# List rows placed by TensorE products, another order ahead of layer 1, and earlier fetches in a three-layer max-aggregation GNN on one Trainium2 core

## The chip, the cores and the metric

The kernel runs on one core of one Trainium2 chip. The core has five engines that work side by side and meet at semaphores: TensorE (PE, matrix products; PEld is its weight load), VectorE (DVE), ScalarE (ACT), GpSimd (POOL, which here mostly issues indirect DMAs: row gathers by a list of indices) and SyncE (SP, which issues the other DMAs). The metric is device time in microseconds (us), the median over several runs. Lower is better.

## The reference, cut to what matters

There are N = 6250 nodes with 128 features and E = 200000 edges, sorted by destination; the destinations are drawn unevenly (6250 times the square of a uniform number), so that some nodes have many edges and most have few. All numbers are float32.

```python
def sage(x, src, dst, Wl, bl, Wr):
    agg = jax.ops.segment_max(x[src], dst, num_segments=x.shape[0])
    agg = jnp.where(jnp.isfinite(agg), agg, 0.0)
    return agg @ Wl + bl + x @ Wr

h = jnp.maximum(_layernorm(x, axis=-1), 0.0)
h = leaky_relu(sage(h, src, dst, Wl1, bl1, Wr1), 0.01)   # 128 -> 256
h = leaky_relu(sage(h, src, dst, Wl2, bl2, Wr2), 0.01)   # 256 -> 256
h = leaky_relu(sage(h, src, dst, Wl3, bl3, Wr3), 0.01)   # 256 -> 128
return x + h
```

## The kernel before

**Tiles and tables.** The nodes are cut into 50 tiles of 127 (`R`). Each layer's input stands in DRAM three times: as rows (`table`, for gathers), as pairs of source tiles (`pair`, 25 pairs `g`) and transposed (`across`). Destination tiles fall into four groups `k`: narrow ones (list 0, 20 tiles), eight virtual ones that hold pieces of the three tiles with the most edges (their rows are found by `virtual`, L446), the remaining 19 narrow ones, and the eight wide ones.

**The main way of an edge.** For each layer, group and source pair there is a step. ACT (or DVE, L1077) makes one-hot matrices (`hot`, L1081 and L1083) from byte indices (`idx_sb`), PE multiplies them with the pair's features (`pg`, L1112), which fetches for every destination one source row, and DVE takes the maximum into `acc` (L1127, L1129). There are 975 steps: 225 in layer 1, 375 in each of the other two. In layer 1 group 0 has steps 0 to 74, the virtual group 75 to 124, group 2 steps 125 to 199 and the wide one the rest.

**The lists.** A source pair serves at most so many edges of one destination. What is left over goes into lists: DVE picks a tile's leftover entries (`pick_rows`, L744, into `picked`), ranks the destinations by their number (`rank_rows`, L774, giving `to_i`, where a destination's entries go, and `end_i`, where its result will stand), and the entries are rearranged so that the longest lists come first and short columns need few gathers. `CAPS` says how many entries each block of 128 destinations has at most; the longest few are folded over free partitions (`fold`). Per entry column, GpSimd gathers 128 rows from `table` (`Listed.gather`, L1174), for which ACT first turns the entries into integers (`let`, L1159). DVE takes the maxima of gathered rows (L1184, L1217), and SP stores the result to `best` (L1224). Layer 1 has 517 such gathers, the others 563 each.

**How list rows are rearranged before the change.** `send_row` (L829) scatters one tile's picked entries to DRAM (`picks`) by an indirect DMA on GpSimd, with a small memset ahead of it: 59 in all, 20, 8, 19, 8 and 4 for lists 0 to 4. `load_ell` (L839) loads the result (`ell`, and its folded part `fold`) back on SP. List 0 is done ahead of layer 1; the others inside it, by chores.

**Ahead of layer 1.** 50 windows (`window`, L386, gather on POOL and count on ACT, L391) find where each tile's edges begin (`places`, L395, giving `at_i`); then `row` (L421) fetches each tile's edge columns on POOL: 39 narrow, 8 wide by `at_i`, 8 virtual by `pos_i`. LayerNorm in five blocks (`ln_...`) runs between. `expand` (L862) and `lookups` (L881) make the byte indices of group 0.

**Nodes.** When a tile's maxima are done, its list result is fetched from `best` as `agg` by POOL (`Node.fetch`, L1244; virtual ones through `Joined`, L1317), transposed on PE (`aT_p`, L1260), joined with `acc` on DVE (`mz`, L1266) and multiplied with the weights (L1271 to L1275).

**What sets the order.** The engines run in program order. The program is written step by step from an agenda: `plan(t, rank, f)` puts a piece of work into step `t`, and within a step the ranks come in a fixed order: first LET, FRESH, TURN, then half the step's products, then MAXIMA, REST, LINEAR, MERGE, SOONER, GATHER and FETCH, then the other half. Chores (masks, flags, picks, ranks, expands, lookups of the later groups) are spread over steps by `spread` (L1448). In layer 1 each gather is put on a step by a planner's clock (`step_us`), the estimated cost of a gather `POOL_US` and a head start `BEHIND_US`. Every gather waits, by an added dependency, for the last maximum written ahead of it (`maxed[-1]`).

## Time and profile before

| | |
|---|---|
| median of 3 runs | 3005.79 us (3004.02 to 3019.61) |
| the profiled execution's own time | 3018.82 us |
| its span in the trace | 3017.0 us |
| mean granted TensorE clock | 0.90 |
| DMA traffic | 594.48 MB, mean 197 GB/s |
| first list gather on POOL | starts at 199.2 us |
| layer 1's last list gather | starts at 1006.4 us |
| layer 2's first list gather | starts at 1220.7 us |

The profile is of one execution. Its groups name a line, an engine, an operation and the tiles (output, then inputs), with a count; then busy time and the mean of one in ns; then the idle time of the engine just before them and what ended most of it. "issue" is time in which the engine waited for nothing that the profile shows. Line numbers are those of the kernel before.

### The profile page before, as it was taken

To read this page: it belongs to the slowest core of one execution; us is meant where nothing else is said; L and a number is where in the kernel's file an instruction comes from. 1 tells how busy PE (TensorE), PEld (TensorE's weight loads), DVE (VectorE), ACT (ScalarE), POOL (GpSimd) and SP (SyncE) were. 2 spreads that over 40 slices of the span, in tenths; PEclk is the share of its full clock that TensorE was granted. 3 is DMA by queue.
4 is the path that set the end of the run, shared out by engine and by line. 5 is a ranking of instruction groups with operands and counts; after the bars stand their busy time and mean duration, and the time that the engine had idled before them with its cause. 6 is when DMAs were issued, how large, how long until landed. Compare 5 with 4: busy or idle time off the path is not lost.

```text
span 3017.0 us, 36583 instructions
## 1 busy us (share of the span) xinstructions
PE 2289.6 (76%) x9364; PEld 1728.3 (57%) x9365; DVE 2430.8 (81%) x4080; ACT 1812.6 (60%) x2826; POOL 2045.6 (68%) x2059
## 2 busy tenths in 40 slices
PE   2025545666656787999988999988999897899886
PEld 1023323344434555777776778766777776678664
DVE  6688856877878686889997678898899897678996
ACT  5227768745556665666665578654656665578641
POOL 6787765777677311677777767774577777767773
PEclk9996667777878898999999999999999999999997
DMA  9425544566545478667677887797667667777884
GB/s 249 146 75 135 141 119 113 156 184 202 151 135 155 151 224 251 216 196 220 201 195 226 249 262 237 241 290 252 195 211 220 195 189 212 215 224 231 245 243 129
DMA packets 378786, 594.48 MB, mean 197 GB/s; under 512 B 77438, under 2 KB 230411, under 8 KB 377929
## 3 DMA queue, kind: packets, MB, share of 16 engines
q1 hardware_dynamic: 250425, 346.88, 36.9%
q0 software_dynamic: 85312, 213.54, 25.8%
q10 hardware_dynamic: 42832, 31.64, 3.2%
q8 instruction: 78, 1.28, 0.2%
q14 instruction: 139, 1.14, 0.1%
HBM read 469.30 MB, written 122.50 MB: 196 GB/s over the span
## 4 chain that ended last, share of the span: by engine, by line
PE 31%; DMA 14%; DVE 13%; issue 7%; POOL 4%; ACT 3%; SPq 0%; DVEq 0%; POOLq 0%; ACTq 0%
PE pg L1112 26%; DVE acc L1129 7%; DMA g<-table,let 6%; DMA agg<-best,end_i 5%; POOL g L1174 4%; PE z_p L1273 2%; PE z_p L1275 2%; DVE g L1184 2%; DVE g L1217 1%; ACT away L1081 1%; DMA pair_sb<-pair 1%; ACT hot L1083 1%; DMA idx_sb<-idx 1%; PE aT_p L1260 1%; DMA agg_v<-best,end_i 1%
## 5 line engine op out<-in xcount | busy, mean ns | idle before, releaser
L1112 PE MATMUL pg<-hot,pair_sb 128*128 128x512 f32 (+2 forms) x7448 | 1984.1, 419 | 294.1 <-ACT hot L1083 118.1
L1174 POOL DMA_INDIRECT g<-table,let x1643 | 1666.7, 1014 | 621.9 <-issue 340.5
L1112 PEld LDWEIGHTS pg<-hot,pair_sb 128*128 128x128 f32 x7448 | 1448.5, 203 | 686.7 <-ACT hot L1083 222.2
L1129 DVE TENSOR_TENSOR acc<-acc,pg 128x1024 f32<-128x1024 f32 (+4 forms) x1179 | 1355.3, 1170 | 242.6 <-PE pg L1112 229.4
L1081 ACT ACTIVATE away<-idx_sb,near 128x1024 uint8<-128x1024 uint8 (+3 forms) x585 | 581.0, 993 | 83.7 <-DMA idx_sb<-idx 40.6
L1083 ACT ACTIVATE hot<-away 128x1024 fp32r<-128x1024 uint8 (+3 forms) x585 | 535.0, 915 | 156.9 <-PE pg L1112 141.0
L1083 ACT ACTIVATE hot<-idx_sb 128x1024 fp32r<-128x1024 uint8 (+3 forms) x594 | 514.2, 886 | 185.8 <-PE pg L1112 181.0
L1244 POOL DMA_INDIRECT agg<-best,end_i x141 | 150.2, 1065 | 238.2 <-PE aT_p L1260 175.8
L1277 ACT COPY s<-z_p 127x256 f32<-127x256 f32 (+1 forms) x150 | 50.2, 335 | 339.4 <-PE z_p L1275 321.0
L1217 DVE TENSOR_TENSOR g<-g 128x1024 f32<-128x1024 f32 (+5 forms) x224 | 225.6, 1007 | 33.2 <-DMA g<-table,let 29.6
L1184 DVE TENSOR_TENSOR g<-g 128x256 f32<-128x256 f32 (+3 forms) x394 | 195.7, 497 | 44.5 <-DMA g<-table,let 24.6
L1260 PE MATMUL aT_p<-ident,agg 128*128 128x128 f32 x250 | 60.2, 309 | 128.3 <-DMA agg<-best,end_i 114.4
L1275 PE MATMUL z_p<-wl,mz 128*128 128x256 f32 (+1 forms) x500 | 122.2, 362 | 31.0 <-DVE mz L1266 30.9
L1273 PE MATMUL z_p<-wr,hT_in 128*128 128x256 f32 (+1 forms) x500 | 138.6, 396 | 7.4 <-DMA hT_in<-across 7.4
L969 ACT COPY hT<-hT_p 128x254 f32<-128x254 f32 x100 | 37.1, 371 | 159.0 <-PE hT_p L967 153.1
L1260 PEld LDWEIGHTS aT_p<-ident,agg 128*128 128x128 f32 x250 | 33.9, 153 | 159.7 <-DMA agg<-best,end_i 84.5
L1266 DVE TENSOR_TENSOR mz<-acc,aT_p 128x256 f32<-128x256 f32 (+1 forms) x141 | 52.3, 371 | 84.6 <-PE aT_p L1260 84.4
L1275 PEld LDWEIGHTS z_p<-wl,mz 128*128 128x128 f32 x500 | 89.7, 208 | 44.7 <-DVE mz L1266 36.3
L1077 DVE TENSOR_SCALAR hot<-idx_sb,beyond 128x1024 fp32r<-128x1024 uint8 x144 | 102.9, 715 | 2.1 <-DMA idx_sb<-idx 2.0
L1273 PEld LDWEIGHTS z_p<-wr,hT_in 128*128 128x128 f32 x500 | 82.4, 208 | 30.1 <-DMA hT_in<-across 9.2
L1159 ACT ACTIVATE let<-ell 128x4 int32<-128x4 int16 (+3 forms) x453 | 81.4, 191 | 6.7 <-DMA g<-table,let 4.2
L831 POOL DMA_INDIRECT picks<-picked,to_i x59 | 64.3, 1089 | 20.3 <-issue 10.0
(298 smaller groups left out, 1195.3 us busy)
## 6 DMA issues: line engine op xcount, KB each, us to landing
pair_sb<-pair SPq DMA_DIRECT2D x394, 256.0 KB
idx_sb<-far SPq DMA_DIRECT2D x48, 616.0 KB
g<-table,let POOLq DMA_INDIRECT x1643
far<-away ACTq DMA_DIRECT2D x198, 128.0 KB
pair<-pr SPq DMA_DIRECT2D x98, 256.0 KB
idx_sb<-idx SPq DMA_DIRECT2D x75, 304.0 KB
idx_sb<-far SPq DMA_DIRECT2D x50, 304.0 KB
best<-g SPq DMA_DIRECT2D x118, 128.0 KB
```

Source lines behind the costliest of these rows:

```text
L1077: nc.vector.tensor_scalar(hot[:, :w], d, beyond, None, op0=OP.is_equal)
L1081: nc.scalar.activation(away, d, AF.Abs, bias=near[:, s : s + 1], scale=1.0)
L1083: nc.scalar.activation(hot[:, :w], d, AF.Relu, bias=1.0, scale=-1.0)
L1112: nc.tensor.matmul(to, pr[:, i, kk * P : (kk + 1) * P], hot[:, o : o + bw], start=((alone or s == 0) and i == 0), stop=((alone or s == sid ...
L1129: maxed.append(nc.vector.tensor_max(to, to, of))
L1174: got = nc.gpsimd.indirect_dma_start(out=self.tiles[q, b, j < 0][:, i, :], out_offset=None, in_=tables[self.layer], in_offset=bass.Indirec ...
L1184: nc.vector.tensor_max(g[:h, :n, :], g[:h, :n, :], g[:h, w - n : w, :])
L1217: nc.vector.tensor_max(base[:, : i + 1, :], base[:, : i + 1, :], g[:, : i + 1, :])
L1244: nc.gpsimd.indirect_dma_start(out=self.agg[:, : self.F], out_offset=None, in_=of, in_offset=bass.IndirectOffsetOnAxis(ap=at, axis=0),)
L1260: nc.tensor.transpose(aT_p[:, i, :], self.agg[:, i * P : (i + 1) * P], ident)
L1273: nc.tensor.matmul(z_p, self.hT[:, i, :], wr[layer][:, i, :], start=False, stop=False)
L1275: nc.tensor.matmul(z_p, self.m[:, i, :], wl[layer][:, i, :], start=False, stop=(i == K - 1))
```

## The change

It has five parts.

1. **List rows are placed by products.** `send_row` and `load_ell` go, and with them `picks`. `place` builds on DVE, for some tiles of a list at a time, a one-hot matrix of each entry's lane and, for every block of 128 destinations, the entries where the block matches and zero elsewhere. `gather_rows` multiplies the two on PE, one product a tile, summed in PSUM, and copies the sum to `ell` (float32 now, with only as many columns a block as `CAPS` allows). `fold_rows` moves the folded columns over partitions by products with shifted identities. Inside layer 1 `move` plans a placement in one step and its products in the next.
2. **Another order ahead of layer 1.** Windows are 200 wide instead of 400 (`WINS` = 8 samples), the first 20 narrow tiles have 32 columns flagged instead of 40 (`CN`). Window gathers, row fetches and LayerNorm pieces are interleaved in another order; `expand` runs for each half of group 0. List 0's rank, placement, products and fold come behind the expands, the lookups and the bias split.
3. **Work put behind the first gathers.** After 12 list gathers come the eight virtual rows, 32 gathers, and then the last six narrow and the eight wide rows. `virtual` runs in step 1, the check of windows in step 2. The floor stores on SP come behind the bias stores.
4. **Early fetches.** FETCH moves from the end of a step to its head. In layers 2 and 3 the nodes of the last group are fetched up to two steps ahead, into six buffers.
5. **Planning.** Chores of the first stretch are spread over steps 7 to 54 instead of 0 to 54. Late lookups are in two parts, the second two steps later. Layer 1's list stores are issued three steps later instead of two. In layer 1 a gather waits for the fourth last maximum instead of the last. `POOL_US` is 1.26 for 1.34, `BEHIND_US` 75 for 62, and the early gathers are counted from 24 us for 10.

```diff
-CB = 40
-WIN = 400
+CB, CN = 40, 32
+WIN, WINS = 200, 8
...
-    def send_row(k, i):
-        nc.gpsimd.memset(gap_t, 0.0)
-        s = nc.gpsimd.indirect_dma_start(
-            out=picks[k], out_offset=bass.IndirectOffsetOnAxis(ap=to_i[k][:, i : i + 1], axis=0),
-            in_=picked[k][:, i, :], in_offset=None,
...
-    def load_ell(k):
-        n = len(LISTS[k])
-        rows = picks[k].rearrange("(p q) m -> p q m", q=n)
-        nc.sync.dma_start(ell[k], rows)
...
+    def parts_of_list(k, most):
+        n, width_k = len(LISTS[k]), sum(RAGGED[k][-1])
+        m = min(n, most // max(P, width_k))
+        m = -(-n // -(-n // m))
+        return [range(i, min(i + m, n)) for i in range(0, n, m)]
+
+    def place(k, us, S, at):
+        n, W = len(us), sum(RAGGED[k][-1])
+        of = slice(us[0], us[-1] + 1)
+        hot, data = S(at[0], F32, n, P), S(at[1], F32, n, W)
+        nc.vector.tensor_tensor(
+            hot, iota_f[:, None, :].to_broadcast([P, n, P]), lane_f[:, of, None].to_broadcast([P, n, P]), op=OP.is_equal
+        )
+        for q, (o, m) in enumerate(RAGGED[k]):
+            nc.vector.scalar_tensor_tensor(
+                data[:, :, o : o + m], block_f[:, of, None].to_broadcast([P, n, m]), float(q), picked[k][:, of, :m],
+                op0=OP.is_equal, op1=OP.mult,
+            )
+        return hot, data
+
+    def gather_rows(k, us, hot, data):
+        W = sum(RAGGED[k][-1])
+        p = psum.tile([P, 512], F32, tag="t", bufs=2, name="ell_p")
+        for i in range(len(us)):
+            nc.tensor.matmul(p[:, :W], hot[:, i, :], data[:, i, :], start=(i == 0), stop=(i == len(us) - 1))
+        if us[0] == 0:
+            nc.scalar.copy(ell[k], p[:, :W])
+        else:
+            nc.vector.tensor_add(ell[k], ell[k], p[:, :W])
+
+    def fold_rows(k):
...
+                nc.tensor.matmul(
+                    p[:, to : to + b - a], moved[d][:h, :], ell[k][:h, a:b], start=(j == 0), stop=(j == len(cuts) - 1)
+                )
...
+        nc.scalar.copy(fold[k], p)
...
-            if maxed:
-                tc.add_manual_dep(got.ins, maxed[-1].ins.name, SYNC, reason="gathers keep to the steps")
+            behind = 1 if self.layer else 4
+            if len(maxed) >= behind:
+                tc.add_manual_dep(got.ins, maxed[-behind].ins.name, SYNC, reason="gathers keep to the steps")
...
-                later_on(2, lambda: nc.sync.dma_start(view[:, q, :], base[:, 0, :]))
+                later_on(2 if self.layer or q == n - 1 else 3, lambda: nc.sync.dma_start(view[:, q, :], base[:, 0, :]))
...
-            self.agg = node.tile([P, H], F32, tag="agg", name="agg", bufs=4)
+            pool, tag, n = (later, "agg_v", 6) if layer and self.k == NK - 1 else (node, "agg", 4)
+            self.agg = pool.tile([P, H], F32, tag=tag, name="agg", bufs=n)
...
+    def move(k, t):
+        for us in parts_of_list(k, 12 * P):
+            got = []
+            plan(t, MAXIMA, lambda us=us, got=got: got.extend(place(k, us, S_acc, (1, 3))))
+            plan(t + 1, MAXIMA, lambda us=us, got=got: gather_rows(k, us, *got))
+            t += 2
+        plan(t, MAXIMA, lambda: known(k))
+        return t
...
-        chores.append((2, lambda: lookups(us, got[0], s, made)))
+        chores.append((2, lambda: got.update(v=leaves(us, got[0], s, made))))
+        behind[len(chores) - 1] = lambda: lookups(us, got["v"], s, made)
...
-                plan(t + 3, MAXIMA, lambda k=k: send(k))
-                plan(t + 9, MAXIMA, lambda k=k: load(k))
-                loaded_in[k] = t + 9
+                loaded_in[k] = move(k, t + 1)
...
-    for (n0, n1), (t0, t1) in zip(itertools.pairwise(parts_at), ((0, 54), (55, 108), (110, 172))):
+    for (n0, n1), (t0, t1) in zip(itertools.pairwise(parts_at), ((7, 54), (55, 108), (110, 172))):
...
-    POOL_US, LAND_US, BEHIND_US = 1.34, 12.0, 62.0
+    POOL_US, LAND_US, BEHIND_US = 1.26, 12.0, 75.0
...
-            plan(ta, FETCH, begin(key, make))
+            plan(ta - ahead, FETCH, begin(key, make))
+            plan(ta, FETCH, lambda: accs[key].load())
...
-    soon = early_list
-    for t in range(EARLY):
-        soon.release(t)
-        soon.gather(t)
-    window_check()
     setup.close()
...
     pair_until(0)
+    load_until(0)
+    halves_of = list(zip(parts_of_list(0, 12 * P), ((1, 3), (0, 2)), strict=True))
+    rank_rows(0, S_acc, made)
+    placed = [place(0, us, S_acc, at) for us, at in halves_of]
+    for (us, _), got in zip(halves_of, placed):
+        gather_rows(0, us, *got)
+    fold_rows(0)
+
+    def early_gathers(t0, t1):
+        for t in range(t0, t1):
+            early_list.release(t)
+            early_list.gather(t)
+
+    early_gathers(0, 12)
+    plan(1, MAXIMA, lambda: virtual(lambda i: acc_t[i // 2][:, 1, i % 2 * 12 * P : (i % 2 + 1) * 12 * P]))
+    plan(2, MAXIMA, window_check)
+    plan(2, GATHER, lambda: [row(("w", NW + v)) for v in range(NV)])
+    plan(2, GATHER, lambda: early_gathers(12, EARLY))
+    plan(4, GATHER, lambda: [row(("n", i)) for i in range(NN - 6, NN)])
+    plan(8, GATHER, lambda: [row(("w", i)) for i in range(NW)])
...
-        act(LET, FRESH, TURN)
+        act(LET, FETCH, FRESH, TURN)
...
-        act(MAXIMA, REST, LINEAR, MERGE, SOONER, GATHER, FETCH)
+        act(MAXIMA, REST, LINEAR, MERGE, SOONER, GATHER)
```

Next, three places in the order of instructions. A row is a line, an operation, its output and inputs with buffer numbers, the output's shape, and how often it comes in a row.

The first is POOL from the first window to the first gathers of layer 1. Before the change, its rows up to the second of the 20 sends (`win_d` is a window, `rows_n` and `rows_w` are edge columns):

```order
L386 DMA win_d<-in_dst_dram,win_i 128x400 x23
L421 DMA rows_n<-cols,at_i 128x48 x20
L386 DMA win_d<-in_dst_dram,win_i 128x400 x27
L421 DMA rows_n<-cols,at_i 128x64 x19
L421 DMA rows_w<-cols,at_i 128x128 x8
L830 MEMSET gap_t 128x1
L831 DMA picks_160<-picked_905,to_i_910 2560x24
```

After the change, from the first window to the long run of gathers ahead of the first node's fetch:

```order
L387 DMA win_d<-in_dst_dram,win_i 128x200 x13
L422 DMA rows_n<-cols,at_i 128x48 x10
L387 DMA win_d<-in_dst_dram,win_i 128x200 x10
L422 DMA rows_n<-cols,at_i 128x48 x10
L387 DMA win_d<-in_dst_dram,win_i 128x200 x27
L422 DMA rows_n<-cols,at_i 128x64 x13
L1205 DMA g<-table_75,let 128x128 x12
L422 DMA rows_w<-cols,pos_i 128x64 x8
L1205 DMA g<-table_75,let 128x128 x32
L422 DMA rows_n<-cols,at_i 128x64 x6
L422 DMA rows_w<-cols,at_i 128x128 x8
L1205 DMA g<-table_75,let 128x128 x208
```

The sends are gone, the 50 windows are cut into three runs with row fetches between, and 22 row fetches stand behind the first 12 list gathers.

The second is SP at the loads that the first products need. Before the change, the last stores of the floors, then list 0's loads and what follows:

```order
L630 DMA joined_149<-zeros 1x128
L630 DMA joined_150<-zeros 1x256
L842 DMA ell_890<-picks_160 128x480
L849 DMA fold_895<-picks_160 64x1 x2
L849 DMA fold_895<-picks_160 32x2 x4
L902 DMA idx_152<-v_1420 25x1024 x2
L902 DMA idx_152<-v_1420 25x512
L556 DMA bias_0_1456<-b_parts 1x16x16 x3
L556 DMA bias_1_1466<-b_parts 1x16x16 x3
L556 DMA bias_2_1476<-b_parts 1x16x8 x3
L1034 DMA pair_sb<-pair_4_82 128x512 x4
L1026 DMA idx_sb<-idx_152 128x2560 x5
```

After the change, the bias stores and the first of the 23 floor and zero stores:

```order
L564 DMA bias_0_1274<-b_parts 1x16x16 x3
L564 DMA bias_1_1284<-b_parts 1x16x16 x3
L564 DMA bias_2_1294<-b_parts 1x16x8 x3
L983 DMA table_75<-floor 1x128
L983 DMA table_76<-floor 1x256
L983 DMA table_77<-floor 1x256
```

The list's loads are gone. The 23 small floor and zero stores, which came before them, now lie between the bias stores and the first four `pair_sb` loads, which follow directly behind the last of them and are followed by the five `idx_sb` loads as before.

The third is DVE where list 0 is ranked and placed after the change, ahead of step 1's virtual rows (`lane_f` and `block_f` say where an entry goes; the tiles named `acc_1342` and `acc_1343` are used as scratch here):

```order
L768 TENSOR_SCALAR rank_h<-left_n_341 128x20
L769 SCALAR_TENSOR_TENSOR rank_f<-to_i_334,rank_h 128x20
L777 TENSOR_SCALAR rank_h<-count_n 128x20
L778 TENSOR_TENSOR rank_f<-rank_f,rank_h 128x20
L780 TENSOR_SCALAR end_i_324<-rank_f 128x20
L783 TENSOR_TENSOR sums<-rank_p,lim_351 128x24
L785 TENSOR_REDUCE over<-sums 128x1
L798 TENSOR_TENSOR acc_1342<-iota_f,lane_f 128x1280
L802 SCALAR_TENSOR_TENSOR acc_1343<-block_f,picked_329 128x10x22
L802 SCALAR_TENSOR_TENSOR acc_1343<-block_f,picked_329 128x10x10
L802 SCALAR_TENSOR_TENSOR acc_1343<-block_f,picked_329 128x10x9
L802 SCALAR_TENSOR_TENSOR acc_1343<-block_f,picked_329 128x10x8 x2
```

Before the change nothing stood between the last row of the rank and the virtual rows; here two comparisons of 128x1280 elements and 44 small products do. The second half is like the one shown, but for its end: the sum of the second product is added to `ell`.

More of the change, by code (lines that the diff above doesn't have):

```diff
@@ L930 @@
     L0 = LISTS[0]
+    half = NP // 2
     list_consts()
-    half = NP // 2
+    for i, b in enumerate((bl1, bl2, bl3)):
+        bias.append(load_b(b, f"b{i + 1}", first))
+    ln_stats(4)
+    ln_stats(3)
+    some(6)
+    ln_root(4)
+    some(1)
+    ln_root(3)
+    some(6)
+    ln_rows(4)
+    places(FIRST, HALF)
+    for i in range(half):
+        row(("n", i))
+    places(0, VT)
+    some(5)
+    ln_relu(4)
+    ln_rows(3)
+    ln_stats(2)
+    some(5)
+    ln_turn(4)
+    ln_root(2)
+    ln_halves(4)
```

272 lines of the change are left out of this document (128 added, 144 removed).

## The prediction

> **What bounds the kernel now.** I read the page first, then busy time by stretches, then each engine's waits, then GpSimd's timeline. The page's first lines (busy time, share of the span, instructions), its clock line and the gather group:
>
> ```profile
> PE 2289.6 (76%) x9364; PEld 1728.3 (57%) x9365; DVE 2430.8 (81%) x4080; ACT 1812.6 (60%) x2826; POOL 2045.6 (68%) x2059
> ...
> PEclk9996667777878898999999999999999999999997
> ...
> L1174 POOL DMA_INDIRECT g<-table,let x1643 | 1666.7, 1014 | 621.9 <-issue 340.5
> ```
>
> No engine is full over the whole span, so the bound must be read stage by stage. The busy time by stretches does that; a row is the stretch, its length, busy time of PE, PEld, DVE, ACT and POOL, then clock and DMA share:
>
> ```profile
> 0.00:100.00 100.00, 17.29 (x64) 11.66 (x64) 68.92 (x369) 52.47 (x119) 66.39 (x68) 1.00 0.92 265
> 100.00:200.00 100.00, 18.59 (x85) 15.93 (x86) 69.46 (x235) 14.80 (x48) 78.72 (x89) 1.00 0.16 40
> 212.00:510.00 298.00, 151.03 (x421) 100.11 (x422) 224.39 (x707) 217.12 (x293) 208.22 (x235) 0.68 0.48 128
> 510.00:1010.00 500.00, 313.33 (x1028) 212.53 (x1027) 387.70 (x795) 278.74 (x424) 379.83 (x384) 0.78 0.56 158
> 1010.00:1190.00 180.00, 148.02 (x575) 102.07 (x573) 145.88 (x208) 131.58 (x180) 23.19 (x23) 0.91 0.74 231
> 1190.00:1605.00 415.00, 385.28 (x1618) 302.50 (x1619) 369.74 (x392) 264.67 (x423) 296.13 (x290) 0.97 0.69 206
> ```
>
> There are four kinds of stage. Setup (to about 200 us) is a chain over DVE, POOL and ACT. From there to 1010 us POOL shows 76%, but each gather is followed by about 0.30 us of issue, so it goes end to end: layer 1 there is bound by GpSimd. From 1010 to 1190 POOL is nearly empty (23 of 180) and DVE and PE set the pace. In layers 2 and 3 PE is at 93% and DVE at 89%. GpSimd's groups between 200 and 1010 us, and the spread of the gather's time there:
>
> ```profile
> L1174 POOL DMA_INDIRECT g<-table,let x517 | 521.1, 1008 | 185.8 <-issue 112.2 <-ACT hot L1083 22.1 <-DMA g<-table,let 15.2
> L831 POOL DMA_INDIRECT picks<-picked,to_i x39 | 39.4, 1011 | 17.1 <-DVE rank_h L806 9.9 <-issue 7.3
> L1174 POOL DMA_INDIRECT g<-table,let x517: 940/945/2316, 199.2 to 1006.4; - x173
> ```
>
> **The change, term by term**, against the profiled execution's 3018.82 us (span 3017.0 and 1.8 around it). That run lies 13.0 over the median 3005.79; I subtract the same difference from the median.
>
> *Setup: the first gather.* GpSimd's timeline (start, duration) around list 0 and DVE's around the virtual rows, which follow list 0's rank; then DVE's two longest waits before 230 us:
>
> ```profile
> 157.77 2.53 POOL L831 DMA_INDIRECT picks<-picked,to_i  x1
> 187.62 1.11 POOL L831 DMA_INDIRECT picks<-picked,to_i  x1 [0.15 <-issue]
> 189.03 1.12 POOL L421 DMA_INDIRECT rows_w<-cols,pos_i  x1 [0.30 <-DVE b_parts L552]
> 199.22 0.95 POOL L1174 DMA_INDIRECT g<-table,let  x1 [0.30 <-issue]
> ...
> 145.10 0.16 DVE L449 TENSOR_SCALAR nrow_i<-count_n 128x3 int32<-128x3 f32 x1
> 156.54 2.26 DVE L500 TENSOR_SCALAR starts<-iota_r,vs,has_v 128x1024 bf16<-128x1024 f32 x3
> 168.18 0.22 DVE L511 TENSOR_SCALAR by_row<-iota_f,part_f 128x8 f32<-128x8 f32 x1
> 171.32 0.16 DVE L526 TENSOR_REDUCE over<-outside 128x1 f32<-128x3 f32 x1
> ...
> DVE at_n L397 <- ACT junk_w L391: 24.3, 3, 18.2
> DVE acc L1662 <- DMA bias<-b_parts: 9.8, 1, 9.8
> ```
>
> Twenty sends (31 us) and eight row fetches (10 us) lie ahead of the first gather; all go from there. But list 0's rank now stands behind the expands, the lookups and the bias split on DVE, with two placements, 20 products and the fold behind it. DVE's work ahead of the first gather is 68.9 + 69.5 = 138 us now. The virtual rows leave it (145.1 to 158.8 and 168.2 to 171.5: 17 us), placement comes (12, below), and ten half expands for five add about 1.5, an estimate: 135. DVE stood idle 62 us of the first 200; windows half as wide shorten its wait for ACT, but now two rounds of row fetches have windows between them. I keep 68 idle: first gather at about 204, **+5**; ends 55 and 95 idle, first gather at 190 and 230 (-9 and +31).
>
> What a placement costs no row shows. Nearest rows, of DVE and, for its products, of PE:
>
> ```profile
> L361 DVE TENSOR_TENSOR pr<-hs,pr 128x1280 fp32r<-128x1280 f32 x5 | 7.4, 1475 | 2.9 <-ACT pr L346 2.9
> L793 DVE TENSOR_TENSOR scratch<-scratch,rank_p 128x500 f32<-128x500 f32 x1 | 0.7, 674 | 1.1 <-PE rank_p L792 1.1
> L398 DVE SCALAR_TENSOR_TENSOR at_n<-win_f,at_n 128x20 f32<-128x20 f32 (+2 forms) x3 | 0.5, 177 | 0.1
> ...
> L1260 PE MATMUL aT_p<-ident,agg 128*128 128x128 f32 x250 | 60.2, 309 | 128.3 <-DMA agg<-best,end_i 114.4
> ```
>
> List 0 is placed in two parts. Each has one 128x1280 comparison (1.48 us) and 22 small products over 1180 elements in all. From 20 elements at 177 ns to 500 at 674 a further element costs about 1.04 ns, so such an instruction has some 0.16 us fixed: 22 x 0.16 + 1.2 = 4.7. Together 6.2 a part, 12 for list 0. The same sum gives about 3 for list 1, 15 for list 2 (three parts), 8 for lists 3 and 4, so **38 us more DVE work** in all, 26 of it behind the first gather. The fixed part may be smaller in a row of small instructions, so I keep 25 and 38 as the ends and take 38. The 59 products are priced by the transposes (309 ns): 18 us of PE, spread over lists; PE has 147 of 298 us idle from 212 to 510, which hides all but list 0's, where about 3 us show between the second placement and the fold (inside the 68). The copies to `ell` and `fold` are ten on ACT of about 0.35 us: nothing.
>
> *GpSimd in layer 1.* Behind the first gather 39 sends go: 39 x (1.01 + 0.30) = -51. Two waits around lists go with them: 9.9 for `rank_h` above, and 19.3 here, where the last gather of list 1 and the first of list 2 stand:
>
> ```profile
> 440.99 1.09 POOL L1174 DMA_INDIRECT g<-table,let  x1 [0.30 <-issue]
> 496.50 1.25 POOL L1174 DMA_INDIRECT g<-table,let  x1 [19.32 <-ACT hot L1083]
> ```
>
> That is -29. In their place 22 row fetches come behind the first gathers (8 by `pos_i`, 6 narrow, 8 wide), 22 x 1.27 (the eight from 189.03 to 199.22 took 10.2) = +28, and after 12 gathers (15 us) POOL waits for `pos_i`, whose 17 us of DVE and 24 small products now start only at step 1: about +10. No step reads them before the late lookups, whose work now starts at step 7 and not at 0, which is their cover. With the start's +5 GpSimd alone would be through with layer 1's lists -51 - 29 + 28 + 10 + 5 = **37 us earlier**.
>
> *What DVE gives back.* Where DVE waited in layer 1, from 212 to 510 us and then from 510 to 1030:
>
> ```profile
> DVE acc L1129 <- PE pg L1112: 25.2, 8, 8.8
> DVE g L1217 <- DMA g<-table,let: 18.6, 4, 8.0
> DVE g L1184 <- DMA g<-table,let: 11.2, 5, 5.1
> ...
> DVE mz L1266 <- PE aT_p L1260: 25.9, 10, 5.8
> DVE mz L1263 <- PE aT_p L1260: 17.4, 3, 14.4
> ```
>
> Up to list 2 DVE has 74 us free of 298, and must now take the virtual rows (17 us) and some 18 us of placements. About half lands on steps that waited for nothing. Also list 1's last gather comes later than its 441 us (rows and `pos_i` ahead of it), so the steps that take its maxima end later, and list 2, whose place is counted in steps, starts at 500 to 515 and not at 477. Only behind that is POOL's freedom felt, and from 1010 on not POOL but DVE and PE set the end. On the other side nodes are fetched at the head of a step, which reaches the 25.9 us of waits for transposes. Of GpSimd's 37 I let one third arrive: **-12**. The ends are -37 (all) and +15 (nothing, and half of the 38 us shows).
>
> *Layers 2 and 3.* PE's waits from 1190 us on:
>
> ```profile
> PE aT_p L1260 <- DMA agg<-best,end_i: 78.7, 42, 6.8
> PE pg L1112 <- DVE acc L1129: 59.3, 68, 3.2
> ```
>
> `agg` fetches move from behind the step's gathers to the head of the step, and the last list's nodes by up to two steps. A wait of 78.7/42 = 1.9 us is shorter than the four or five gathers (1.3 us each) that stood ahead, so most could go. But DVE is at 89% there and PE waits for it already; and each fetch only changes places with gathers on POOL. I take 12 of the 79, **-12**, nearest to the row that says DVE is late next; ends 0 and -30.
>
> *Nothing, with cover.* The floor stores on SP now lie ahead of the first pair loads. SP's rows for them, the bias and the loads:
>
> ```profile
> 88.55 4.02 SPq L624 DMA_DIRECT2D table<-floor  x3
> 99.97 0.54 SPq L630 DMA_DIRECT2D joined<-zeros  x2
> 194.67 5.65 SPq L556 DMA_DIRECT2D bias<-b_parts  x9
> 202.57 1.77 SPq L1034 DMA_DIRECT2D pair_sb<-pair  x4
> ```
>
> The floors take 12 us of SP. With the split done near 170, bias and floors are through before 190, and list 0 is ready only at 204. Without that cover it would be up to 12. Lookups in two pieces, best stores a step later and gathers bound to the fourth last maximum only loosen waits. Sum: 3018.82 - 12 - 12 = 2994.8; for the median 3005.79 - 24 = **2982**.
>
> A rule against the change. Gathers of layer 1 take 945 ns in the median and 1008 in the mean, so 63 ns x 517 = 33 us lie above the usual time, beside 612 us of DVE work; by that, 26 us more DVE work costs POOL 1.4. The Trainium skill, page "SBUF — State Buffer", section "Who interferes with whom", says that a VectorE instruction with two SBUF inputs takes the port through which GpSimd reads, and that the one that comes second is fully blocked. By that rule all 26 us of placements could hold gathers back (rival D); the trace agrees only for the 33 us.
>
> **The rivals.**
> A. GpSimd's gain arrives in full and the node waits go: -37 - 25 = -62, 2944. For it: POOL end to end from 200 to 1010. Against: 1010 to 1190 belongs to DVE, and list 2 starts by steps. Chance 0.14.
> B. No change: DVE's 38 us eat the gain in layer 1 (0), and in layers 2 and 3 DVE, late next, leaves 3: 3003. For it: DVE is the busiest engine, and at 78% up to 1010. Against: 74 us free up to 510. Chance 0.25.
> C. Slower: list 0 becomes the setup's end. Its rank waits behind the expands, so that every us by which the chain exceeds 204 shifts all gathers. At 95 us of DVE idle the first gather comes at 230, 26 behind my estimate, and nothing else in layer 1 hides it: -24 + 26 in sum is even; with layer 1's 12 given back to DVE and the `pos_i` wait doubled (+10) it is +24, 3030. It turns slower from a first gather at about 220. Against: DVE was through with list 0's rank at 145. Chance 0.15.
> D. The placements hold GpSimd's gathers back one for one: 26 us off the 37 leaves 11, of which a third arrives (-4), and layer 2's lists, started late, leave 2 of the 12 there: -6, 3000. For it: one gather took 2316 ns for 945. Against: the mean of 1008. Chance 0.04.
>
> **How the numbers follow.** The forecast has 0.42; by its terms' smaller errors it spans 2965 to 2997. 0.5% of the median, 15 us, is about what a measurement of this kernel can tell from no change: faster is below 2991, slower above 3021. The forecast gives 0.35 to faster and 0.07 to same; A 0.14 to faster; B 0.02 to faster, 0.22 to same and 0.01 to slower; C 0.03 to same, 0.12 to slower; D 0.04 to same. Faster 0.51, same 0.36, slower 0.13. The range reaches to A's middle (half of its 0.14 left out) and to 3028, short of C's middle (some 0.08 left out): 2944 to 3028.
>
> **What would show it.** First gather between 200 and 210 and first sends gone: the setup term; at 220 or later, C. A gap of about 10 us on POOL behind the twelfth gather, then 8 row fetches. List 2's first gather at 500 to 515, and layer 1's last at 970 to 1000 for 1006: the GpSimd term. DVE's busy share between 212 and 510 up from 75% to some 85%. PE's wait for `agg` in the later layers below 70 us. Placement instructions whose sum is far from 38 us, or gathers with a mean well over 1008 ns, would make it wrong, and so would layer 2 beginning no earlier although POOL is through earlier.

## The result, and the profile after

The changed kernel takes 3020.72 us (median of 14 runs, 3015.48 to 3032.58), the kernel before 3005.55 beside it (14 runs, 2995.57 to 3019.61): a ratio of 1.0053, 95% interval 1.0037 to 1.0068. So it is **slower by 0.5%**, some 15 us, where 24 us faster was forecast. The profiled execution has a span of 3023.5 us. It lies 5 us above its median and that of the kernel before 13 us above its own, so the two traces differ by only 6.5 us. One execution of `after_both` (10745 us) and one of the kernel before in the fifth group (3058 us) stand far above their neighbours and are left out of the ratios below.

First the same views as before. The page's busy times and the gather group of the changed kernel:

```profile
PE 2308.4 (76%) x9548; PEld 1748.3 (58%) x9549; DVE 2452.6 (81%) x4259; ACT 1805.7 (60%) x2836; POOL 1973.9 (65%) x1941
...
L1205 POOL DMA_INDIRECT g<-table,let x1643 | 1678.4, 1022 | 663.0 <-issue 343.5
```

GpSimd did lose its work: 2045.6 us became 1973.9. VectorE took 22 us more. The busy time by stretches of the changed kernel, same columns as before:

```profile
0.00:100.00 100.00, 7.77 (x36) 6.24 (x36) 61.97 (x343) 23.18 (x63) 52.98 (x58) 1.00 0.51 115
100.00:200.00 100.00, 24.00 (x114) 17.62 (x114) 69.44 (x303) 35.62 (x98) 37.08 (x38) 1.00 0.45 153
212.00:510.00 298.00, 150.75 (x451) 105.91 (x453) 219.78 (x717) 173.24 (x242) 193.66 (x193) 0.64 0.41 109
510.00:1010.00 500.00, 324.19 (x1058) 223.44 (x1056) 400.58 (x864) 293.14 (x445) 374.29 (x360) 0.78 0.57 159
1010.00:1190.00 180.00, 146.31 (x600) 102.29 (x600) 145.17 (x227) 130.88 (x175) 29.63 (x30) 0.95 0.69 202
```

In setup POOL's busy time fell by 55 us, and nothing came earlier for it. Between 212 and 510 us DVE is no fuller than before (219.8 us for 224.4): it waits as much as it did, and its larger work takes more time. GpSimd's timeline of the changed kernel, at the first list gather, the rows by `pos_i`, the last gather of list 1, and the first of list 2:

```profile
199.34 0.94 POOL L1205 DMA_INDIRECT g<-table,let  x1 [17.83 <-ACT let L1190]
...
223.44 0.94 POOL L422 DMA_INDIRECT rows_w<-cols,pos_i  x1 [6.54 <-DVE rem L523]
...
473.27 0.94 POOL L1205 DMA_INDIRECT g<-table,let  x1 [0.30 <-issue]
526.28 1.37 POOL L1205 DMA_INDIRECT g<-table,let  x1 [52.07 <-ACT let L1190]
```

The first gather starts where it did (199.22 before). List 1's last is 32 us later than before (440.99), list 2's first 30 us later (496.50), and ahead of it GpSimd now stands idle for 52 us where it stood idle for 19. What the sends had cost has become waiting. Step by step (the end of a step's last maximum, from the trace): the changed kernel lies 1.6 us behind the old one at the first step, 34 at step 44, 41 at step 53, 31 at the end of layer 1, 30 at step 424 and 11 at the last step. So **the loss is made in the first 53 steps**; it is 51 at step 165, and 18 us of it come back at one place (33 at step 171), and 20 in layers 2 and 3. A second trace of the changed kernel, `after_again` below, agrees with this one within about 3 us up to the end of layer 1, but lies 9 us earlier at the last step: what is read from single traces for layers 2 and 3 is good to some 10 us. The place where 18 us come back is this wait in the kernel before:

```profile
997.56 0.94 POOL L1244 DMA_INDIRECT agg<-joined,last_i  x1 [0.30 <-issue]
1000.54 0.29 DVE L1263 COPY mz<-aT_p 128x128 f32<-128x128 f32 x1 [14.38 <-PE aT_p L1260]
```

DVE waits there for the transpose of a virtual node's list result, which GpSimd starts to fetch only at 997.56 us, behind gathers and the four sends of list 4. Here GpSimd's lighter load did pay. The question is what made the 41.

### The profile page after: what moved, and what is told of

It is laid out like the page before. It is cut to its first block, busy times and chain, and to the rows that moved or that the text cites. A ratio compares the mean times of both kernels' runs of the same rounds, so it can differ in the third digit from the quotient of the medians.

```text
span 3023.5 us, 36942 instructions
## 1 busy us (share of the span) xinstructions
PE 2308.4 (76%) x9548; PEld 1748.3 (58%) x9549; DVE 2452.6 (81%) x4259; ACT 1805.7 (60%) x2836; POOL 1973.9 (65%) x1941
## 4 chain that ended last, share of the span: by engine, by line
PE 35%; DVE 18%; DMA 16%; issue 8%; POOL 4%; ACT 4%; SPq 0%; DVEq 0%; ACTq 0%; POOLq 0%
PE pg L1143 28%; DVE acc L1160 9%; DMA g<-table,let 6%; DMA agg<-best,end_i 4%; POOL g L1205 4%; ACT away L1112 2%; DVE g L1216 2%; PE z_p L1309 2%; DVE g L1249 2%; PE z_p L1311 2%; ACT hot L1114 1%; DMA pair<-pr 1%; DMA pair_sb<-pair 1%; DMA agg_v<-best,end_i 1%; PE hT_p L998 1%
## 5 line engine op out<-in xcount | busy, mean ns | idle before, releaser
L1190 ACT ACTIVATE let<-ell 128x4 int32<-128x4 f32 (+3 forms) x453 | 81.4, 192 | 14.2 <-DMA g<-table,let 14.0
L422 POOL DMA_INDIRECT rows_n<-cols,at_i x39 | 38.3, 982 | 61.9 <-DVE at_i L402 50.9
```

## The experiments

The runs fell on two kinds of chip: on some the kernel before takes 3005 to 3009 us, as above, on others 3455 to 3491. A time is therefore compared only with runs of its own group; "of before" is the ratio to the kernel before on the same chip, with its 95% interval. In the expectations, theory V (VectorE) and theory G (GpSimd) say which engine sets the pace up to step 53; theory O (order) looks for the loss in parts 2 and 3, theory P (planner) in part 5.

### First group (kernel before 3491.06 us there)

`after_rows`: 14 row fetches back ahead of the first gathers.

```diff
-    for i in range(NEAR, NN - 6):
+    for i in range(NEAR, NN):
         row(("n", i))
+    for i in range(NW):
+        row(("w", i))
...
-    plan(4, GATHER, lambda: [row(("n", i)) for i in range(NN - 6, NN)])
-    plan(8, GATHER, lambda: [row(("w", i)) for i in range(NW)])
```

> The changed kernel, but the 14 row fetches by at_i that stand behind list gathers (6 narrow, 8 wide) go back ahead of the first gather, where GpSimd stands idle from 181.5 to 199.3 us. Theory V (VectorE): up to step 53 the pace is DVE's work plus its idle time ahead of the first step, so list 1's last gather comes 18 us earlier than 473.3 but list 2's first stays at 526 within 5 us, and the time at 3021 within 6. Rival G (GpSimd): the steps wait for list 1's gathers, list 2's first gather comes 12 to 18 us earlier, and the time is 3003 to 3009.

`after_place`: placements repeated.

```diff
+            for _ in range({1: 3, 2: 1}.get(k, 0)):
+                plan(t, MAXIMA, lambda us=us: place(k, us, S_acc, (1, 3)))
             plan(t, MAXIMA, lambda us=us, got=got: got.extend(place(k, us, S_acc, (1, 3))))
```

> The changed kernel, with list 1's placement done four times instead of once (3 x about 2.4 us more of DVE, near 292 us) and list 2's twice (about 10.5 us more, at 489 to 513 us). Theory V: all 18 us arrive, list 2's first gather moves from 526 to 541-546, and the time from 3021 to 3033-3039. Rival G: GpSimd is idle for 52 us there, so list 1's extra work is swallowed, list 2's first gather comes at most 11 us later, and the time stays within 6 of 3021.

`after_setup`: two pieces of DVE's work put elsewhere ahead of layer 1.

```diff
     ln_root(2)
+    mask_rows(L0[:half], S_first)
+    flag_rows(L0[:half], S_first)
     ln_halves(4)
...
-    mask_rows(L0[:half], S_first)
-    flag_rows(L0[:half], S_first)
...
-    sorted_check()
...
     pick_rows(0, half, L0[half:NP], S_first)
+    sorted_check()
```

> The changed kernel with two things in setup put elsewhere on DVE: the check that edges are sorted (it waits 10.4 us for PE) goes behind the second half's picks, and masks and flags of the first ten row fetches go ahead of the first pair halves (which wait 15.7 us for ACT). Theory V: DVE's chain to the first step loses 10 to 20 us of idle time, first gather at 180-190 instead of 199.3, list 2's first at 508-516, time 3003 to 3011. Rival G: the first gathers come earlier too, but list 1 still ends behind its row fetches; list 2's first moves by at most 6, the time by at most 6.

`before_fetch`: part 4 alone on the kernel before (the hunks on FETCH, `load` and the six buffers).

> The kernel before with nothing of the change but part 4 (FETCH at the head of a step, the last group's nodes up to two steps ahead). In the changed kernel the lag behind the old one falls from 31 us at the end of layer 1 to 11 at the end. If that is the early fetches' doing, this kernel gains about 20 us in layers 2 and 3 and some 5 in layer 1: 2980 to 2988. Rival: the later layers' gain came with the other list positions or the planner, and this stands within 6 us of 3005.

Measured: 3552.44 (1.019 of before, 1.012 to 1.026), 3567.37 (1.023, 1.016 to 1.029), 3553.98 (1.019, 1.013 to 1.026) and 3510.50 (1.006, 1.003 to 1.010). The changed kernel itself had no run there, so only the three can be set beside each other: with the placements repeated list 2's first gather starts at 632 us, against 608 and 612 in the other two, and the time is 14 us higher. Theory V had 15 to 20 us later and 12 to 18 us more time, so this speaks for it; but list 2's own placement lies on list 2's own chain, and with four executions each the 14 us are barely clear of the noise. Early fetches alone did not pay there; they cost 0.6%.

### Second group (kernel before 3006.37 us)

> The changed kernel as it is, as the yardstick for the runs beside it: the first four experiments ran where the kernel before takes 3491 us and not 3005, so that their lists and steps have no trace of the changed kernel to stand beside. Both theories: 1.005 of the kernel before on a chip like the first (1.004 to 1.007). On one like the second, theory V (DVE's chain) puts it between 1.017 and 1.021, since the row fetches and the setup order then made little difference there; theory G (list 1's late gathers) above 1.021.

3020.75, 1.0038 (1.0018 to 1.0058): as measured first.

`before_place`: part 1 alone. The functions `place`, `gather_rows`, `fold_rows`, `move` and the ragged `ell` stand in the kernel before; ahead of layer 1:

```diff
-    for i in range(len(L0)):
-        send_row(0, i)
-    load_ell(0)
+    for us in parts_of_list(0, 12 * P):
+        gather_rows(0, us, *place(0, us, S_first, (0, 1)))
+    fold_rows(0)
```

> The kernel before with nothing of the change but part 1: all five lists placed by products, no sends, no list loads; order ahead of layer 1, planner and fetches as before. Theory V: DVE's 38 us of placement go into the steps before list 3 (12 in setup, 14 up to step 53) while the 31 us of sends ahead of the first gather come off only in part, since DVE sets the first step; later 15 us come back where list 3's load was waited for. Time within 10 us of the kernel before (ratio 0.997 to 1.003). Theory G: 83 us of sends leave GpSimd, which bounds layer 1, and the time falls by 25 to 50 us (0.983 to 0.992).

3001.97, 0.9977 (0.9958 to 0.9995). Theory V's time; taking some 82 us of sends from GpSimd brought little on the whole. But V's way there was only half right: the first step ends 13.5 us later than in the kernel before and step 53 still 13.1, so the 13 us of placement behind the first step were swallowed (DVE's idle time between the two steps fell from 66.9 to 53.4 us). The 13.5 us come back between steps 165 and 171 (14.7 us behind, then 3.0 ahead), at the wait for `joined` shown above.

`after_both`: the edits of `after_rows` and `after_setup` together.

> The changed kernel with both earlier edits: 14 row fetches back ahead of the first gather, and the sorted check and the first half's masks and flags moved in setup. Theory V: DVE's idle time ahead of the first step falls by 10 to 20 us and list 2's first gather by as much against the changed kernel; ratio to it 0.993 to 0.997. Theory G: list 2's first gather falls by 15 to 30, ratio 0.990 to 0.995. Neither: if the rows' masks are not the chain, it is within 0.2% of the changed kernel.

3010.59, 1.0001 (0.9983 to 1.0019), 10 us under the changed kernel. The first step is where it was (228.5 for 231.0 us), so the edit in setup gave nothing: DVE's wait only moved. What is left are the row fetches: list 1's last gather starts at 461.8 for 475.9 and list 2's first at 516.1 for 529.5. For these 10 us theory G had the way right, but both its sizes (15 to 30 us, 0.990 to 0.995) were too large; V had the size, by a way that did not occur. The row fetches alone had no run on this kind of chip.

`after_fetch_late`: part 4 undone.

```diff
-        act(LET, FETCH, FRESH, TURN)
+        act(LET, FRESH, TURN)
...
-        act(MAXIMA, REST, LINEAR, MERGE, SOONER, GATHER)
+        act(MAXIMA, REST, LINEAR, MERGE, SOONER, GATHER, FETCH)
...
-                       min(every * j, 2) if layer and k == NK - 1 else 0)
+                       0)
```

> The changed kernel with part 4 undone (FETCH at the end of a step again, nothing fetched ahead). If the 20 us by which the changed kernel catches up in layers 2 and 3 are the early fetches' doing, it loses them: ratio to the changed kernel 1.005 to 1.009, and PE's wait for agg rises by 15 to 25 us. Rival: the early fetches do nothing there (the kernel before with them alone stood at 1.006 of the kernel before on the second chip), and it stays within 0.2%.

3042.30, 1.0117 (1.0096 to 1.0138): the early fetches are worth 21.5 us in the changed kernel, 0.7% for the 0.5 to 0.9% forecast. From layer 2's start to the last step it catches up 7 us on the kernel before where the changed kernel beside it catches up 27. PE's wait for `agg` is 70.1 us, against 54.3 in `after_again` beside it and 65.2 in the changed kernel's first trace. A row that differs by 11 us between two executions of one kernel can't tell how much of the gain lies in it.

### Third group (kernel before 3454.89 us) and fourth (3456.15 us)

`place_fetch`: parts 1 and 4 together on the kernel before.

> The kernel before with parts 1 and 4 alone (lists by products, early fetches), order ahead of layer 1 and planner as before. If the parts add up: placement alone stood at 0.998 of the kernel before, and taking part 4 out of the changed kernel cost 21.5 us, so 2978 to 2990, ratio 0.990 to 0.995, faster than both kernels. Rival: the fetches pay only where lists come late, and this stands within 0.3% of the kernel before.

`place_fetch_plan`: part 5 on top of it.

```diff
-            if maxed:
-                tc.add_manual_dep(got.ins, maxed[-1].ins.name, SYNC, reason="gathers keep to the steps")
+            behind = 1 if self.layer else 4
+            if len(maxed) >= behind:
+                tc.add_manual_dep(got.ins, maxed[-behind].ins.name, SYNC, reason="gathers keep to the steps")
...
-                later_on(2, lambda: nc.sync.dma_start(view[:, q, :], base[:, 0, :]))
+                later_on(2 if self.layer or q == n - 1 else 3, lambda: nc.sync.dma_start(view[:, q, :], base[:, 0, :]))
...
-((0, 54), (55, 108), (110, 172))
+((7, 54), (55, 108), (110, 172))
...
-    POOL_US, LAND_US, BEHIND_US = 1.34, 12.0, 62.0
+    POOL_US, LAND_US, BEHIND_US = 1.26, 12.0, 75.0
```

The late lookups in two parts, not shown, are in it too. The early gathers are still counted from 10 us, so that one piece of part 5 is missing here.

> The same with part 5 too (chores from step 7, lookups in two pieces, stores a step later, gathers bound to the fourth last maximum, POOL_US 1.26, BEHIND_US 75), so that only parts 2 and 3, the order ahead of layer 1, are left of the difference to the changed kernel. Theory O (order): the some 40 us that the changed kernel has lost against parts 1 and 4 alone come from parts 2 and 3; this stays within 8 us of parts 1 and 4 alone (2978 to 2998). Theory P (planner): they come from the later gathers and chores of part 5; this stands at 3010 to 3025.

`after_split`: `after_both` with a `yield` in `virtual` ahead of `by_row`, its two pieces in steps 1 and 2, and 8 more gathers ahead of the rows by `pos_i`.

> The changed kernel with the two earlier edits in setup and the virtual rows in two pieces again, a step apart, as the kernel before had them; 8 more gathers stand ahead of the rows by pos_i. In the changed kernel DVE waits 7.1 + 1.9 us for PE inside the virtual rows, ahead of the first step's maximum. Theory O: these 9 us go, the first step's maximum and list 2's first gather (516 us there) come 7 to 10 us earlier, 3000 to 3005 (0.997 of the run without the split). Rival: PE's products are what the first step waits for and the wait only moves; within 3 us of 3010.

`after_clock`: `after_both` with the clock's three constants back (1.34, 62.0 and 10).

> The changed kernel with the two earlier edits in setup and only the planner's clock constants as before (POOL_US 1.34, BEHIND_US 62, early gathers counted from 10 us). Theory P: gathers are planned some 13 us, that is two or three steps, earlier, list 1's last gather (462 us there) does not move since GpSimd is busy without a break, but maxima are planned earlier, DVE waits longer for gathers, and the time rises or falls by 5 to 15 us. Theory O: within 4 us of 3010.

Third group: 3455.44 (0.9998, 0.9972 to 1.0025), 3517.12 (1.0173, 1.0125 to 1.0221), 3514.05 (1.0186, 1.0144 to 1.0228), 3487.40 (1.0114, 1.0074 to 1.0153). Parts 1 and 4 were no faster than the kernel before there, and part 5 cost 62 us. `after_clock` is 27 us under `after_split`, but the two differ by the clock's constants and by the split of the virtual rows, and `after_both` had no run there, so the share of neither can be told. As this was again the slower kind of chip, three of these kernels and `after_place` ran once more:

> Parts 1 and 4 alone on the kernel before, once more, for a chip like the first. If the parts add up as measured there (placement 0.998, fetches worth 21.5 us): 2975 to 2988, 0.990 to 0.994 of the kernel before. If the fetches pay only where lists come late (on the second chip this stood at 1.000): 0.996 to 1.000.

> Parts 1, 4 and 5, once more, for a chip like the first. Theory O (order ahead of layer 1, parts 2 and 3): within 8 us of parts 1 and 4 alone; list 2's first gather stays near the 503 us of placement alone. Theory P (planner, part 5): 3005 to 3025, 25 to 45 us above parts 1 and 4 alone, most of it lost before list 2's first gather.

> The changed kernel with the two edits in setup and the planner's clock as before, once more. Theory P: 10 to 20 us below the 3010.6 of the same without the clock's edit (there 0.7% was gained on the second chip against its neighbours). Theory O: within 5 us of 3010.6.

> The changed kernel with list 1 placed four times and list 2 twice (about 18 us more DVE work ahead of list 2's first gather), once more, beside the changed kernel's own 3020.75. Theory V: list 2's first gather at 541 to 546 for 526 to 529, time 3033 to 3039. If DVE's waits for gathers swallow it, as they did for placement alone: first gather below 537, time below 3030.

The fourth group was of the same kind: 3456.27 (1.0024), 3513.81 (1.0190), 3492.35 (1.0101) and 3544.30 (1.0259). It repeats the third (part 5: 58 us) and adds nothing on the first kind of chip.

### Fifth group (kernel before 3009.18 us)

> Parts 1 and 4 alone. Where the kernel before takes about 3005 us: 2975 to 2988 if the parts add up (0.990 to 0.994), 2997 to 3005 if the fetches pay only where lists come late. Where it takes about 3450: 0.998 to 1.004, as measured twice.

> Parts 1, 4 and 5. Where the kernel before takes about 3005 us: theory O within 8 us of its neighbour (parts 1 and 4), list 2's first gather near 503 us; theory P 25 to 45 us above it, list 2's first gather at 520 to 535. Where it takes about 3450: 55 to 65 us above its neighbour, as measured twice.

Parts 1 and 4: **2984.80 us, 0.9936 (0.9913 to 0.9959), faster than both kernels**. With part 5: 3014.11, 1.0012 (0.9992 to 1.0031). **Part 5 costs 29 us** by the medians and 23 by the ratios, about the low end of the 25 to 45 that theory P gave, and list 2's first gather comes at 523.6 us, in its window. Theory O is out. Parts 2 and 3, with the early gathers' count, have the rest: some 7 us by the medians to the changed kernel's 3020.75, 10 when each is set against the kernel before beside it.

Where part 5 loses them, the busy time by stretches shows, each time from the start to the end of the first step's maximum, and from there to list 2's first gather. The kernel before:

```profile
0.00:227.40 227.40, 40.16 (x159) 30.29 (x160) 161.90 (x647) 82.39 (x183) 166.11 (x178) 0.99 0.56 156
227.40:496.50 269.10, 136.43 (x388) 90.86 (x388) 199.60 (x651) 189.12 (x258) 186.57 (x213) 0.68 0.47 125
```

The changed kernel:

```profile
0.00:229.00 229.00, 49.92 (x217) 39.07 (x218) 146.29 (x685) 75.04 (x187) 107.94 (x111) 0.94 0.46 126
229.00:526.30 297.30, 147.49 (x439) 103.03 (x440) 227.98 (x751) 178.02 (x247) 185.35 (x187) 0.65 0.42 112
```

Parts 1 and 4 (`c_place_fetch`):

```profile
0.00:241.30 241.30, 51.71 (x211) 41.38 (x212) 170.20 (x690) 82.96 (x185) 141.48 (x142) 0.83 0.51 148
241.30:503.00 261.70, 151.28 (x454) 104.42 (x454) 208.35 (x710) 182.72 (x256) 153.88 (x155) 0.69 0.45 122
```

Parts 1, 4 and 5 (`c_place_fetch_plan`):

```profile
0.00:232.00 232.00, 50.99 (x208) 41.15 (x210) 147.73 (x647) 73.26 (x175) 133.84 (x135) 0.84 0.51 146
232.00:523.60 291.60, 154.17 (x443) 105.70 (x443) 225.96 (x745) 188.46 (x259) 162.62 (x163) 0.66 0.43 115
```

The third number of busy time is DVE's. Part 5 takes 22.5 us of DVE's work out of the time ahead of the first step (170.2 to 147.7), but the first step ends only 9.3 us earlier: the work had stood beside waits. Behind it DVE has 17.6 us more to do up to list 2's first gather, and waits 12.3 us more (291.6 - 226.0 against 261.7 - 208.4). That is +29.9 behind the first step and -9.3 ahead of it: 20.6 us, by which list 2's first gather is late. The changed kernel's rows read like the last two. Which work it is, DVE's timeline shows around the first maxima (`acc<-pg`). In parts 1 and 4, the first and the last instruction of the masks and flags of the eight virtual tiles, then the maxima:

```profile
216.61 0.63 DVE L703 TENSOR_TENSOR acc<-iota_f,rem 128x512 int16<-128x512 f32 x1
239.68 0.48 DVE L748 TENSOR_TENSOR rows_w<-rows_w,acc 128x504 int16<-128x504 int16 x1
240.09 2.84 DVE L1156 COPY acc<-pg 128x1024 f32<-128x1024 f32 x3
```

With part 5, the first maximum, then the same masks and flags, and what DVE and ACT do behind them:

```profile
230.75 1.22 DVE L1161 COPY acc<-pg 128x1024 f32<-128x1024 f32 x1 [13.11 <-PE pg L1146]
243.82 0.68 DVE L703 TENSOR_TENSOR acc<-iota_f,rem 128x512 int16<-128x512 f32 x1
266.68 0.43 DVE L748 TENSOR_TENSOR rows_w<-rows_w,acc 128x504 int16<-128x504 int16 x1
267.02 0.28 DVE L1219 TENSOR_TENSOR g<-g 128x128 f32<-128x128 f32 x1
267.33 0.91 ACT L1226 COPY g<-g 32x128 f32<-32x128 f32 x3 [17.92 <-DVE g L1219]
```

Without part 5 these 23 us of work stand ahead of the first maximum, where DVE would wait for PE's first products anyway; with it DVE waits 13.1 us there, and does the work in one block in front of later maxima. The kernel before has the masks ahead of the first maxima as well:

```profile
212.91 3.08 DVE L685 TENSOR_TENSOR acc<-acc 128x496 int32<-128x496 int32 x5
218.74 3.08 DVE L685 TENSOR_TENSOR acc<-acc 128x496 int32<-128x496 int32 x5
226.21 2.84 DVE L1127 COPY acc<-pg 128x1024 f32<-128x1024 f32 x3
```

In the changed kernel, at the same place, stand the virtual rows:

```profile
215.45 0.22 DVE L519 TENSOR_SCALAR acc<-iota_f,part_f 128x8 f32<-128x8 f32 x1
222.80 0.17 DVE L520 TENSOR_TENSOR acc<-of_p,acc 128x8 f32<-128x8 f32 x1 [7.13 <-PE of_p L503]
227.77 1.21 DVE L1158 COPY acc<-pg 128x1024 f32<-128x1024 f32 x1
```

In the kernel before these masks and flags (L685 and its neighbours) are chores of step 0. The changed kernel, whose virtual rows come only now, waits 7.1 us for PE there, and does the same masks from 235.1 to 259.1 us, behind the first maxima. The second share is waits. Of DVE's 12.3 us more, 4.4 are for gathers (32.3 for 27.9), 4.0 for PE's products (20.6 for 16.6), and the rest small. GpSimd's timeline in parts 1 and 4, at list 1's last gather and list 2's first:

```profile
443.73 1.19 POOL L1203 DMA_INDIRECT g<-table,let  x1 [0.30 <-issue]
503.04 0.94 POOL L1203 DMA_INDIRECT g<-table,let  x1 [58.12 <-ACT let L1188]
```

With part 5, at a wait inside list 0 and at the same two places:

```profile
269.94 1.26 POOL L1208 DMA_INDIRECT g<-table,let  x1 [17.73 <-ACT away L1115]
470.52 0.94 POOL L1208 DMA_INDIRECT g<-table,let  x1 [0.30 <-issue]
523.59 1.36 POOL L1208 DMA_INDIRECT g<-table,let  x1 [52.12 <-ACT let L1193]
```

With part 5 GpSimd stands still for 17.7 us in the middle of list 0, and list 1 ends 27 us later. This wait, too, is the masks' doing: GpSimd waits for ACT, and ACT waits 17.9 us for the maximum of gathered rows that DVE takes at 267.02, right behind the block. Both kernels then leave it idle for 52 to 58 us: list 2 starts by steps, not by GpSimd. The account of the 20.6 us is 13.2 of work that lost its cover (22.5 - 9.3) and 12.3 of waits, less 4.9 of work not yet done at that point (22.5 - 17.6); by the end of step 53 these have come too (25 us), and the last 4 of the 29 follow later. So the trace shows the late start of the chores at both ends: the little it gains ahead of the first step, and what it costs behind. No run on the first kind of chip takes the chores' start and the planner's clock apart, so how much of the 29 each has stays open.

## Why the prediction was wrong

**The step that failed** is the one that cost part 5 at nothing. The prediction said of the row fetches that "no step reads them before the late lookups, whose work now starts at step 7 and not at 0, which is their cover", and of the rest that it would "only loosen waits". Starting at step 7 was no cover but the price: the masks and flags of step 0 stood beside ACT's and PE's work ahead of the first maxima, and from step 7 they stand in front of maxima. The planner's constants were not priced at all. Runs with and without part 5 put this at 29 us by the medians (23 by the ratios), in place of 0. The row fetches themselves were priced, at 28 us of GpSimd, and their cover failed too: putting 14 of them back ahead of the first gather went with 10 us less time.

**A second step** failed beside it: that a third of GpSimd's gain arrives in layer 1. Without part 5 nothing of it does. That parts 1 and 4 alone then come out at -24.4 us by the medians (2984.80 for 3009.18; -19 by the ratio), next to the forecast's -24, is luck: the forecast has 12 of it in layer 1, where the trace shows none, and it was for all five parts.

Point by point, by the prediction's own steps:

- *First gather at about 204, +5.* It came at 199.34. In the first 200 us DVE worked 131 us and stood idle 69, for the 135 and 68 of the sum: nearly right.
- *38 us of placement on DVE.* Right in its order, at the low end of 25 to 38. The comparisons and the products of the changed kernel:

```profile
L802 DVE SCALAR_TENSOR_TENSOR acc<-block_f,picked 128x60 f32<-128x60 f32 (+36 forms) x117 | 17.4, 224 | 0.0
L798 DVE TENSOR_TENSOR acc<-iota_f,lane_f 128x1280 f32<-128x1280 f32 (+4 forms) x8 | 9.1, 1133 | 0.0
L816 DVE TENSOR_TENSOR ell<-ell,ell_p 128x211 f32<-128x211 f32 (+1 forms) x3 | 1.0, 340 | 3.5 <-PE ell_p L812 2.7 <-ACT away L1112 0.7
```

  27.5 us in all: the small instructions overlap, 17.4 us of time for 117 of 224 ns each. List 0 has 20 of them a part and 40 in all, not 22 and 44; that is less than 1 us of its 12.
- *GpSimd through with layer 1's lists 37 us earlier.* Its items were there (39 sends gone, 22 row fetches added, 6.5 us of wait for `pos_i` instead of 10), but the 29 us of waits around lists did not go. They grew to the 52.07 shown, and the last gather starts at 1016.8 us, 10 later and not 37 earlier. Even in parts 1 and 4, where it starts at 989.1, 17 earlier, layer 2's first list gather stands at 1221.9 for 1220.7: layer 2 begins no earlier although GpSimd is through earlier, the prediction's own sign of being wrong. From list 2's first gather to the last GpSimd did gain: 490.5 us for 509.9.
- *List 2's first gather at 500 to 515; DVE 85% busy between 212 and 510.* 526 and 74%. The reading that layer 1 is "bound by GpSimd" from 200 to 1010 us was the wrong ground: up to step 53 neither engine is full alone. DVE's work and its waits for gathers add up, so work that moves into these steps costs up to its length, while work that leaves GpSimd gains little when the gathers are planned by steps.
- *-12 in layer 1.* +31. Without part 5 the end of layer 1 is level with the kernel before (+1 us in `c_place_fetch`), so a third of GpSimd's 37 was too much as well. There the 17.6 us that GpSimd's lighter load gave near step 168 only paid for the 13.9 by which list 0's placement made the first step late.
- *-12 in layers 2 and 3.* By the traces -20 in the changed kernel (-26 in `after_again`), -27 with parts 1 and 4, and -11 with placement alone, all against one trace of a long execution of the kernel before, so good to some 10 us. By the medians the early fetches are worth 21.5 us in the changed kernel, and the traces of `after_fetch_late` and `after_again` put nearly all of them behind layer 1. Right in sign, and probably too small. PE's wait for `agg`, of the changed kernel, from 1190 us on:

```profile
PE aT_p L1296 <- DMA agg<-best,end_i: 65.2, 35, 4.6
PE pg L1143 <- DVE acc L1160: 60.9, 72, 3.4
```

  It fell below 70 as forecast, from 78.7 (54.3 in `after_again`), and DVE's share stayed level; where the rest of the gain lies was not traced further.
- *The rivals.* A (GpSimd's gain in full) is refuted by placement alone at 0.9977. B had the size nearest to the truth for placement (nothing in layer 1). C was the forecast slower case, but its mechanism, a late first gather, did not occur. D was hardly put to the test. Of the 27 us of placement 8 stand ahead of the first gather, and all of list 2's in the 58 us in which GpSimd is idle, so that in `before_place` only six of layer 1's 517 gathers meet a placement at all. These six took 1431 ns in the mean, the others 1011. One of them, with the comparison beside it:

```profile
767.69 1.22 DVE L847 TENSOR_TENSOR acc<-iota_f,lane_f 128x1024 f32<-128x1024 f32 x1
767.76 1.96 POOL L1203 DMA_INDIRECT g<-table,let  x1 [0.30 <-issue]
```

  As the Trainium skill has it, page "SBUF — State Buffer", section "Who interferes with whom", a VectorE instruction with two SBUF inputs contends with a GpSimd instruction that reads SBUF, and the port pair they share is an exclusive lock. The long gathers beside placements agree with that, but come to some 2.5 us in all. The mean of all 517 rose from 1008 to 1016 ns with placement alone, and to 1033 and 1020 in the changed kernel's two traces, where three and two gathers meet a placement. Those 6 to 13 us of GpSimd the prediction did not have, and their cause was not traced.

## What to carry to other kernels

A step that is moved out of an idle stretch costs its length where it lands, and gains in the old place only what did not stand beside a wait: price both ends by the busy and idle time of the engine, not by the stretch's total. Taking work from the engine that looks full brings little when the start of its next batch is set by a schedule; look for the wait that will take its place. A change of five parts is best split before it is believed: two of them made this kernel 0.6% faster, and a third, the start of some chores and a few numbers of a planner, gave more than that back.

## What the runs showed of the hardware that was not expected

The same kernel before took 3005 to 3009 us on some chips and 3455 to 3491 on others, 15% more, and the parts of the change had other sizes there (part 5 58 to 62 us for 29, parts 1 and 4 together 1.000 and 1.002 for 0.994). The granted TensorE clock differed less, 0.85 to 0.87 for 0.90. All twelve traces from the slower kind show DVE waiting for something that the profile calls "remote", at the main line of maxima alone for 145 to 251 us, and for "issue" (59 to 106 us there); the eight traces from the other kind have no "remote" wait at all. In `before_fetch`:

```profile
DVE acc L1129 <- PE pg L1112: 292.1, 216, 6.0
DVE acc L1129 <- remote: 215.5, 74, 8.4
DVE acc L1129 <- issue: 67.0, 85, 6.1
```

What lies behind these waits was not settled. On the slower kind the early fetches alone cost 0.6%; they had no run alone on the other.
